# Fused attention and non-local block: a third nested product for q and k, PSUM read by halves, k's maxima in theta/phi, ScalarE for the last scaling

## The chip, the cores and the metric

The kernel runs on one NeuronCore of one Trainium2 chip. The metric is the device time of one execution in microseconds (us). The profile comes from one further execution of the same program; its span is 2154.5 us. Matrix products run on TensorE (PE in the profile, PEld for its weight loads), elementwise work and reductions on VectorE (DVE), activations and copies on ScalarE (ACT), some products and the accumulating DMAs on GpSimd (POOL), and the DMA queue is fed by SyncE (SP).

## The reference, cut to what matters

There are two layers over eight images of 512 channels and 32 x 32 positions, all in float32. The first is attention with eight heads over 1024 positions, with 1x1 convolutions for q, k, v and the output. The second is a non-local block, followed by a normalization over the whole batch.

```python
# layer 0, x is (8, 512, 32, 32), heads h = 8, d = 64
q = conv1x1(x, Wq, bq); k = conv1x1(x, Wk, bk); v = conv1x1(x, Wv, bv)
attn = softmax(einsum('bhdn,bhdm->bhnm', q, k) * d ** -0.5, axis=-1)
x = x + conv1x1(einsum('bhnm,bhdm->bhdn', attn, v), Wp, bp)
# layer 1, C_INTER = 256, n = 1024
g_x, theta_x, phi_x = (conv1x1(x, w, b) for w, b in (g, theta, phi))
y = einsum('bcd,bdn->bcn', einsum('bcn,bdn->bcd', theta_x, phi_x) / n, g_x)
z = conv1x1(y, W_w, W_b) + x
mean, var = z.mean((0, 2, 3)), z.var((0, 2, 3))      # over all eight images
out = (z - mean) * rsqrt(var + 1e-5) * gamma + beta
```

The mean and the variance need all eight images, so no output can be written before the last image's z is there.

## The kernel before: the parts that the change touches

A 512 x 512 convolution over 1024 positions is taken as a product of two 2 x 2 block matrices and done with seven block products in place of eight (the Winograd form of Strassen's scheme). Blocks of the weights are 256 x 256, blocks of the data 256 channels x 512 positions. `w[:, i]` holds the seven weight blocks: 0 is a11, 1 is a12, 2 is a22, 3 to 6 are the sums s1 to s4; t1 to t4 are the sums of data blocks, made on VectorE. Each entry of `SEVEN` is a product: its weight block, its data block, the PSUM slot that it accumulates in, and the output quarters that read the slot after it. A slot is two PSUM banks, and there are four, rotated through the list `free`.

```python
    SEVEN = (("11", 0, "11", 0, (("11", True),)), ("s1t1", 3, "t1", 1, (("22", True),)),
             ("s2t2", 4, "t2", 0, (("12", True),)), ("s4", 6, "22", 1, (("12", False),)),
             ("s3t3", 5, "t3", 0, (("22", False),)), ("12", 1, "21", 2, (("11", False),)),
             ("t4", 2, "t4", 0, (("21", True),)))
...
    FIVE = (SEVEN[0], SEVEN[1], SEVEN[2], SEVEN[3], ("s3t3", 5, "t3", 0, (("22", False), ("21", False))))
```

For q and k (images 1 to 7) and for the output projection (images 1 to 6) two of the seven, `("12", 1, "21")` and `("t4", 2, "t4")`, are left out of the list, which makes it `FIVE`, and are done by seven products again, of half the size in each direction: 128 x 128 weights with 256 positions. That is `nested`. From the second product of the list on, one such step is given to TensorE after each plain matmul, and each step is followed by one read of its PSUM slot, by VectorE (`add`) or ScalarE (`first`, where the target is written for the first time).

```python
    INNER = (1, 2)
...
    def nested(name, stage, w, data, tags, first, add):

        slots = [bank(tag, f"{name}_in_{tag}") for tag in tags]
        for n, (q, di, begins) in enumerate((("11", "21", False), ("21", "t4", True))):
            a, d = inner_blocks(w, stage, n), data[f"inner {di}"]
            pair = slots if n == 0 else slots[::-1]
            begun = set()
            for _, wi, di, s, reads in SEVEN:
                ps = pair[s % 2 if s < 2 else 1][:, s // 2, n * 256:(n + 1) * 256]
                pe(nc.tensor.matmul(ps, a[wi], d[di], start=s not in begun, stop=True, skip_group_check=True))
                ...   # the reads of this slot, then:
                yield

    def seven(name, w, data, positions_out, first, add, between=None, early=False,
              by_chunk=False, inner=None):
        ...
        for n, (what, wi, di, s, reads) in enumerate(FIVE if inner else EARLY if early else SEVEN):
            ...
            for to_ps, at, lhsT, rhs, k in work:          # four matmuls 128x512, or eight 128x256
                pe(nc.tensor.matmul(to_ps, lhsT(k), rhs(k), start=(s, at) not in begun, stop=(k == nk - 1),
                                    skip_group_check=True))
                begun.add((s, at))
                if n:
                    next(steps, None)
            for to, is_first in reads:
                (first if is_first else add)(to, ps)
            if between and n in between:
                between[n]()
```

`pe` and `dve` pin an instruction to program order on its engine; what is not pinned is placed by the scheduler. `block` gives out a tile of 128 x 1024 from a ring of ten, which also holds the exponentials of the attention, the sums t1 to t4 and the inner sums.

After q, k and v of the next image come the projection and then theta and phi of the current one. The maxima of |q| and |k| (`peaks`, four reductions over 1024 each) go into `bound_scores`, which has a small matmul, pinned on TensorE after product 3 of theta/phi, and gates q ahead of the next attention:

```python
        def peaks():
            for c in range(CC):
                ins = nc.vector.tensor_reduce(peak[:, c:c + 1], t[:, c, :], AX.X, ALU.max, apply_absolute_value=True)
                if b == 0:
                    dve(ins)
...
    def bound_scores(b, q, k, peak_q, peak_k):

        nc.vector.tensor_tensor(peak_q, peak_q, peak_k, ALU.mult)
        ps = next_bank(f"bound_{b}")[:, 0, :]
        pe(nc.tensor.matmul(ps[:, :CC], heads, peak_q, start=True, stop=True))
...
        if not last:                                       # in the loop over the images
            inner_sums(nxt["data"], "21", dve)
            more_sums(nxt["data"], (3, 4), dve)
            later = []
            q, peak_q = heads_of(b + 1, "q", ..., inner="WqT", later=later,
                                 between={1: lambda: inner_sums(nxt["data"], "t4", dve)})
            v = values(b + 1, ..., {1: norm, 2: later[0], 5: lambda: nxt["products"]()})

            def sums_of_o():
                nxt["o"] = data_sums(quarters_of(o), f"o_{b}")
                if b:
                    inner_sums(nxt["o"], "21")

            k, peak_k = heads_of(b + 1, "k", ..., inner="WkT", between={2: sums_of_o})
            if b:
                inner_sums(nxt["o"], "t4")
        ...
        tp = theta_phi(b, weights("tp"), data, {} if last else {3: lambda: bound_scores(b + 1, q, k, peak_q, peak_k)})
```

The end, where three images get their z late, channel chunk by channel chunk (`oc`), and every chunk of all eight images is scaled and written:

```python
    def last_z():
        order = [B - LATE, B - 1, *range(B - LATE + 1, B - 1)]
        begun = None
        for oc in range(CC):
            for n, b in enumerate(order[:-1] if oc == 0 else order):
                for h0, h1 in ((0, 1), (1, 2)) if (oc, n) == (CC - 1, LATE - 1) else ((0, NH),):
                    finish_one = n == 0 and begun
                    late_unit(b, oc, h0, h1, (lambda: finish(oc - 1, *begun)) if finish_one else lambda: None)()
            begun = begin(oc)
        finish(CC - 1, *begun)
...
        for i, b in enumerate(sorted(z)):                  # in finish(oc, gs, shift)
            t = z[b][oc]
            if i == 0 or oc == CC - 1 and i % 2 == 0:
                dve(nc.vector.tensor_scalar(t, t, gs, shift, ALU.mult, ALU.add))
            else:
                nc.scalar.activation(t, t, AF.Identity, bias=shift, scale=gs)
            nc.sync.dma_start(out_v[b, :, oc, :], t)
```

Of the kernel before, what the change touches and what calls it, by code (L numbers as in the profile page):

```python
# [30 lines left out]
def unshifted(ctx: ExitStack, tc: tile.TileContext, a: dict, out: bass.AP):  # L31
# [22 lines left out]
    fold1 = ctx.enter_context(tc.tile_pool(name="fold1", bufs=1))  # L54
# [59 lines left out]
    INNER = (1, 2)  # L114
    WIDTH = 7 * C + len(INNER) * 3 * P
# [40 lines left out]
    def inner_blocks(w, name, n):  # L156

        a = w[:, INNER[n]]
        extra = rest[name][:, n * 3 * P:(n + 1) * 3 * P].rearrange("p (i f) -> p i f", i=3)
        return [a[:, 0, :P], a[:, 1, :P], a[:, 1, P:], a[:, 0, P:], extra[:, 0], extra[:, 1], extra[:, 2]]  # L160

    def keep_inner(name, w):

        for n in range(len(INNER)):
            a11, a12, a22, a21, s2, s3, s4 = inner_blocks(w, name, n)
            for to, l, r, op in ((s3, a11, a21, ALU.subtract), (a21, a21, a22, ALU.add), (s2, a21, a11, ALU.subtract),
                                 (s4, a12, s2, ALU.subtract)):
                nc.vector.tensor_tensor(to, l, r, op)
        kept[name] = dram.tile([P, WIDTH], F32, tag=f"kept_{name}", name=f"kept_{name}")
        nc.sync.dma_start(kept[name][:, :14 * w.shape[3]], w.rearrange("p i k f -> p (i k f)"))  # L170
        nc.sync.dma_start(kept[name][:, 14 * w.shape[3]:], rest[name])
# [30 lines left out]
    def inner_sums(data, which, pin=lambda ins: None):  # L202

# [3 lines left out]
        pin(nc.vector.tensor_tensor(t[:, 0], b12, b11, ALU.subtract))  # L207
        pin(nc.vector.tensor_tensor(t[:, 1], b22, t[:, 0], ALU.subtract))
        pin(nc.vector.tensor_tensor(t[:, 2], b22, b12, ALU.subtract))
        pin(nc.vector.tensor_tensor(t[:, 3], b21, t[:, 1], ALU.subtract))  # L210
        data[f"inner {which}"] = {"11": b11, "21": b21, "22": b22, **{f"t{i + 1}": t[:, i] for i in range(4)}}

# [14 lines left out]

    def nested(name, stage, w, data, tags, first, add):

        slots = [bank(tag, f"{name}_in_{tag}") for tag in tags]  # L230
        for n, (q, di, begins) in enumerate((("11", "21", False), ("21", "t4", True))):
            a, d = inner_blocks(w, stage, n), data[f"inner {di}"]
            pair = slots if n == 0 else slots[::-1]
            begun = set()
            for _, wi, di, s, reads in SEVEN:
                ps = pair[s % 2 if s < 2 else 1][:, s // 2, n * 256:(n + 1) * 256]
# [8 lines left out]
    def seven(name, w, data, positions_out, first, add, between=None, early=False,  # L245
              by_chunk=False, inner=None):
# [7 lines left out]
        steps = iter(())  # L254
# [3 lines left out]
        for n, (what, wi, di, s, reads) in enumerate(FIVE if inner else EARLY if early else SEVEN):  # L258
# [14 lines left out]
            for to_ps, at, lhsT, rhs, k in work:  # L273
# [3 lines left out]
                if n:  # L277
                    next(steps, None)
            for to, is_first in reads:
                (first if is_first else add)(to, ps)  # L280
# [64 lines left out]
    def heads_of(b, what, w, bias, data, pin=lambda ins: None, later=None, **how):  # L345
# [18 lines left out]
        def peaks():  # L364
            for c in range(CC):
                ins = nc.vector.tensor_reduce(peak[:, c:c + 1], t[:, c, :], AX.X, ALU.max, apply_absolute_value=True)
                if b == 0:
                    dve(ins)
# [35 lines left out]
    def attention(b, q, k, v, near_end, make_f=None):  # L404
# [66 lines left out]
        def spread(u, pin=lambda ins: None, meanwhile=lambda: None):  # L471
# [4 lines left out]
            if not make_f:  # L476
                acc = accs.pop(u).rearrange("p j n -> p (j n)")
                if u == 0:
                    folded["t"] = foldp.tile([P, 4, 1024], F32, tag="fold", name=f"fold_{b}")
                t = folded["t"]  # L480
                together(t[i * P // 4:(i + 1) * P // 4, g, :],
                         [acc[k * P // 4:(k + 1) * P // 4, :] for k in range(4)])
                if i == 3:
                    two = t[:, g, :].rearrange("(r s) n -> s r n", s=2)
                    together(t[g * D:(g + 1) * D, 2, :], [two[0], two[1]])
                if u == len(units) - 1:
                    folded["all"] = t[:, 2, :]
                return
            if i == 0:
                folded[g] = foldp.tile([P, 4, 1024], F32, tag="fold", name=f"fold_{b}_{g}")  # L490
            acc = accs.pop(u).rearrange("p j n -> p (j n)")
            for k in range(4):
                eng = nc.scalar if make_f and u == len(units) - 1 and k % 2 else nc.sync
                eng.dma_start(folded[g][i * P // 4:(i + 1) * P // 4, k, :], acc[k * P // 4:(k + 1) * P // 4, :])
            if i == 3:
                t = folded[g]
                meanwhile()
                if g == 0:
                    folded[g] = fold1.tile([P, 1, 1024], F32, tag="fold1", name=f"fold1_{b}")
                for part_of in fold_parts(g, t, pin):  # L500
                    part_of()

        def fold_parts(g, t, pin):
            return [lambda to=to, l=l, r=r: pin(nc.vector.tensor_tensor(to, l, r, ALU.add)) for to, l, r in (
                (t[:, 0], t[:, 0], t[:, 1]), (t[:, 2], t[:, 2], t[:, 3]), (folded[g][:, 0], t[:, 0], t[:, 2]))]

        def all_denominators(ps):

            t = folded.pop("all")
# [8 lines left out]
        def denominators(g, ps):  # L518

            t = folded.pop(g)  # L520
            columns(ps, folds, lambda j: t[:, 0, j * 512:(j + 1) * 512])
            alone = make_f and g == 1
            ri = (fold1.tile([P, 1, 1024], F32, tag="fold1", name=f"ri_{b}") if alone else t)[:, 0, :512]
            nc.vector.reciprocal(ri, ps)
            if alone:
# [187 lines left out]
    def late_unit(b, oc, h0=0, h1=NH, meanwhile=lambda: None):  # L713
# [9 lines left out]
        def sums():  # L723
# [3 lines left out]
            meanwhile()  # L727
# [3 lines left out]
        return sums  # L731

    def last_z():
        order = [B - LATE, B - 1, *range(B - LATE + 1, B - 1)]
        begun = None
        for oc in range(CC):
            for n, b in enumerate(order[:-1] if oc == 0 else order):
                for h0, h1 in ((0, 1), (1, 2)) if (oc, n) == (CC - 1, LATE - 1) else ((0, NH),):
                    finish_one = n == 0 and begun
                    late_unit(b, oc, h0, h1, (lambda: finish(oc - 1, *begun)) if finish_one else lambda: None)()  # L740
            begun = begin(oc)
        finish(CC - 1, *begun)
# [8 lines left out]
    def finish(oc, gs, shift):  # L751
# [4 lines left out]
        for i, b in enumerate(sorted(z)):  # L756
            t = z[b][oc]
            if i == 0 or oc == CC - 1 and i % 2 == 0:
                dve(nc.vector.tensor_scalar(t, t, gs, shift, ALU.mult, ALU.add))
            else:  # L760
                nc.scalar.activation(t, t, AF.Identity, bias=shift, scale=gs)
            nc.sync.dma_start(out_v[b, :, oc, :], t)
# [26 lines left out]
    for b in range(B):  # L789
# [5 lines left out]
        def near_end():  # L795
            if not last:
                nxt["data"] = data_sums(quarters_of(nxt["x"]), f"x_{b + 1}", (1, 2))
            elif "data" not in nxt:
# [11 lines left out]
        if not last:  # L810
            inner_sums(nxt["data"], "21", dve)
            more_sums(nxt["data"], (3, 4), dve)
            later = []
            q, peak_q = heads_of(b + 1, "q", weights("WqT"), bq, nxt["data"], dve, inner="WqT",
                                 later=later,
                                 between={1: lambda: inner_sums(nxt["data"], "t4", dve)})
# [13 lines left out]
            k, peak_k = heads_of(b + 1, "k", weights("WkT"), bk, nxt["data"], inner="WkT", between={2: sums_of_o})  # L830
# [3 lines left out]
        else:  # L834
# [3 lines left out]
            between = {4: late_unit(b - 1, 0)}  # L838
# [21 lines left out]
        tp = theta_phi(b, weights("tp"), data, {} if last else {3: lambda: bound_scores(b + 1, q, k, peak_q, peak_k)})  # L860
        load_w(nc.sync)

        def before_wf():
            if last:
                z[b] = [xt[:, cc, :] for cc in range(CC)]
                take_back(B - LATE + 1)
                reload(4, mats, "o")
# [232 lines left out]
```

## Time and profile before

| | before |
|---|---|
| time, median of 3 | 2156.76 us (2156.75 to 2157.21) |
| span of the profiled execution | 2154.5 us |
| TensorE busy | 2128.9 us |
| VectorE busy | 1356.6 us |
| ScalarE busy | 741.4 us |
| one image in the steady part, from one q stage to the next | 264.4 us |

A matmul in float32 appears as two records in the profile, so "x8" in a line of 128x512 matmuls stands for four of them. An instruction's line gives its start and its duration; on VectorE the next one can start a little ahead of the end that is given, so the distance between two starts is the cost in a sequence. Times of TensorE are best read from start to start too[...].

### The profile page before, as it was taken

The page shows a single profiled execution, that of the slowest core. Times are in us where ns is not written, and L with a number is a line of the kernel's source. Part 1 is how long each engine was busy: PE and PEld are TensorE (multiplying, and loading weights), DVE is VectorE, ACT ScalarE, POOL GpSimd, SP SyncE. Part 2 cuts the span into 40 slices and gives each one's busy share as a digit, 9 for nine tenths or more (in the row PEclk, how much of TensorE's full clock was granted, in tenths as well). Part 3 has the DMA queues.
Part 4 walks back from the last instruction along what each step waited for, and adds up shares of the span by engine and source line. Part 5 has one row for each costly group of instructions (what it writes and reads, how often), then busy time and mean ns, then how long its engine had stood idle before and what let it go on. Part 6 is the DMA issues. An engine that isn't in the chain of part 4 may idle for free.

```text
span 2154.5 us, 29726 instructions
## 1 busy us (share of the span) xinstructions
PE 2128.9 (99%) x12426; PEld 1106.9 (51%) x12426; DVE 1356.6 (63%) x1562; ACT 741.4 (34%) x848; POOL 184.9 (9%) x235
## 2 busy tenths in 40 slices
PE   9999999999999999999999999999999999999995
PEld 4534664356733567335663366633666336643462
DVE  5466656666476664766747667476673665657736
ACT  1464104631046310463105621066212652056115
POOL 0111100110001100011000100011000110000000
PEclk9999999999999999999999999999999999999998
DMA  6333434333143331433323342233434334121648
GB/s 217 130 46 59 140 152 126 49 76 118 69 130 50 74 116 68 133 50 79 108 97 109 49 96 99 91 106 50 103 141 147 43 46 133 52 65 40 223 183 351
DMA packets 52941, 226.80 MB, mean 105 GB/s; under 512 B 9664, under 2 KB 16064, under 8 KB 45248
## 3 DMA queue, kind: packets, MB, share of 16 engines
q1 hardware_dynamic: 42128, 197.82, 27.4%
q0 software_dynamic: 9184, 25.70, 9.9%
q8 instruction: 99, 1.62, 0.3%
q10 hardware_dynamic: 1488, 1.32, 0.2%
q14 instruction: 42, 0.34, 0.1%
HBM read 138.03 MB, written 45.88 MB: 85 GB/s over the span
## 4 chain that ended last, share of the span: by engine, by line
PE 98%; DVE 1%; ACT 1%; DMA 0%; issue 0%
PE ps L430 20%; PE po L456 20%; PE pv L274 9%; PE ptp L274 9%; PE pp L274 7%; PE pk L274 7%; PE pq L274 6%; PE pg L274 4%; PE pf L609 3%; PE pz L274 2%; PE pk_in_s L237 2%; PE pq_in_s L237 2%; PE pp_in_s L237 2%; PE pz L720 2%; PE pwf L644 1%; PE den L402 0%
## 5 line engine op out<-in xcount | busy, mean ns | idle before, releaser
L433 ACT ACTIVATE e<-ps 128x1024 f32<-128x1024 f32 x512 | 522.9, 1025 | 428.0 <-PE ps L430 422.5
L439 DVE TENSOR_TENSOR acc<-acc,e 128x1024 f32<-128x1024 f32 x384 | 470.0, 1224 | 141.9 <-ACT e L433 137.3
L456 PE MATMUL po<-e,v 64*64 64x512 f32 x4096 | 528.7, 589 | 0.7 <-ACT w_WgT L611 0.7
L430 PE MATMUL ps<-q,k 64*64 64x512 f32 x4096 | 529.1, 589 | 0.0
L456 PEld LDWEIGHTS po<-e,v 64*64 64x64 f32 x4096 | 156.4, 133 | 283.5 <-issue 275.4
L430 PEld LDWEIGHTS ps<-q,k 64*64 64x64 f32 x4096 | 155.5, 133 | 284.1 <-issue 275.1
L469 POOL DMA_DIRECT2D fold<-acc x168 | 131.1, 780 | 893.1 <-DMA fold<-acc 562.7
L437 DVE TENSOR_TENSOR acc<-e,e 128x1024 f32<-128x1024 f32 x64 | 78.3, 1224 | 139.6 <-ACT e L433 132.9
L632 ACT ACTIVATE g<-pg,gb 128x512 f32<-128x512 f32 x31 | 21.3, 687 | 384.1 <-PE pg L274 381.3
L274 PE MATMUL pv<-w_WvT,t_x 128*128 128x256 f32 x512 | 116.4, 381 | 0.0
L274 PE MATMUL ptp<-w_tp,t_x 128*128 128x256 f32 x512 | 115.0, 380 | 0.0
L274 PEld LDWEIGHTS pv<-w_WvT,t_x 128*128 128x128 f32 x512 | 96.6, 190 | 18.5 <-issue 5.7
L274 PEld LDWEIGHTS ptp<-w_tp,t_x 128*128 128x128 f32 x512 | 96.7, 190 | 12.9
L274 PE MATMUL pp<-t_o,w_WpT 128*128 128x512 f32 x208 | 100.8, 592 | 0.0
L274 PE MATMUL pq<-t_x,w_WqT 128*128 128x512 f32 x200 | 98.8, 593 | 1.0 <-DVE w_WqT L772 1.0
L274 PE MATMUL pk<-t_x,w_WkT 128*128 128x512 f32 x200 | 98.9, 592 | 0.0
L385 ACT COPY v<-pv 128x1024 f32<-128x1024 f32 x32 | 32.4, 1012 | 185.2 <-PE pv L274 185.2
L397 POOL TENSOR_SCALAR q<-q,gates 128x1024 f32<-128x1024 f32 x32 | 35.2, 1111 | 659.8 <-DVE gates L395 659.8
L274 PE MATMUL ptp<-w_tp,x 128*128 128x256 f32 x384 | 86.8, 379 | 0.0
L274 PE MATMUL pv<-w_WvT,x 128*128 128x256 f32 x384 | 86.8, 379 | 0.0
L274 PEld LDWEIGHTS ptp<-w_tp,x 128*128 128x128 f32 x384 | 73.0, 190 | 13.3 <-issue 3.6
L274 PEld LDWEIGHTS pv<-w_WvT,x 128*128 128x128 f32 x384 | 73.0, 190 | 13.3 <-issue 3.6
(187 smaller groups left out, 2191.0 us busy)
## 6 DMA issues: line engine op xcount, KB each, us to landing
fold<-acc POOLq DMA_DIRECT2D x168, 128.0 KB, 3.1
r<-den_d SPq DMA_DIRECT2D x32, 512.0 KB, 6.9
x<-in_x_dram SPq DMA_DIRECT2D x31, 512.0 KB, 6.0
w_WqT<-kept_WqT SPq DMA_DIRECT2D x7, 2176.0 KB, 8.9
w_WkT<-kept_WkT SPq DMA_DIRECT2D x7, 2176.0 KB, 8.7
w_WpT<-kept_WpT SPq DMA_DIRECT2D x6, 2176.0 KB, 8.4
w_WvT<-kept_WvT SPq DMA_DIRECT2D x7, 1792.0 KB, 7.2
w_tp<-kept_tp SPq DMA_DIRECT2D x7, 1792.0 KB, 8.5
```

Of the source, the lines that this page charges most:

```text
L237: pe(nc.tensor.matmul(ps, a[wi], d[di], start=s not in begun, stop=True, skip_group_check=True))
L274: pe(nc.tensor.matmul(to_ps, lhsT(k), rhs(k), start=(s, at) not in begun, stop=(k == nk - 1), skip_group_check=True))
L385: seven(f"pv_{b}", w, data, True, lambda q, ps: nc.scalar.copy(at(q), as_v(ps)), lambda q, ps: dve(nc.vector.tensor_tensor(at(q), at(q), a ...
L397: nc.gpsimd.tensor_scalar(q[:, p, :], q[:, p, :], gate[:, p:p + 1], 1.0, ALU.mult, ALU.mult)
L430: pe(nc.tensor.matmul(ps[c * P // 2:(c + 1) * P // 2, j, :], k[r, p, keys], q[r, p, h * 512:(h + 1) * 512], start=True, stop=True, skip_gr ...
L433: nc.scalar.activation(e, ps, AF.Exp, scale=SCALE)
L437: nc.vector.tensor_tensor(accs[u], es[u, 0], e, ALU.add)
L439: ins = nc.vector.tensor_tensor(accs[u], accs[u], e, ALU.add)
L456: pe(nc.tensor.matmul(ps[j * D:(j + 1) * D, r, :], v[keys, m, (2 * p + j) * D:(2 * p + j + 1) * D], e[keys, j, :], start=(m == 0), stop=(m ...
L469: nc.gpsimd.dma_start(to, part_of, accum_op=ALU.add)
L609: pe(nc.tensor.matmul(ps[:, c, :], tp[:, i, c * P:(c + 1) * P], tp[:, i, CI:], start=(i == 0), stop=(i == NB - 1)))
L720: pe(nc.tensor.matmul(ps[:, h - h0, :], wf[:, d, oc * P:(oc + 1) * P], g[d][:, h * 512:(h + 1) * 512], start=(d == 0), stop=(d == IC - 1), ...
```

## The change

A third of the seven products of q and k, s4 times b22, is also done by seven smaller ones; the output projection keeps two. With that the plain list of q and k shrinks from `FIVE` to `FOUR`, in which s1t1 is read into both quarters 22 and 12. Their plain slots are read as soon as each half (128 x 512) is complete. `STEPS` says how many nested steps follow each plain matmul. The VectorE sums are placed at given matmuls of the q stage by `fills`, and one more set of inner sums, of b22, is made at the end of the attention. k's maxima move from the end of the k stage into theta/phi, after product 1; the sums of o move from after product 2 to after product 1 of the k stage. At the end, the oldest late chunk is done ahead of the last image's Wf, each channel chunk is finished as soon as its statistics are there, and its first image is scaled by ScalarE in two halves (in the last chunk VectorE keeps every other image). Two smaller parts are in the denominators: in the last image the folding of the sums uses accumulating DMAs for all units but the last, as it does in the other images, and a buffer (`fold1`) goes.

```diff
-    INNER = (1, 2)
-    WIDTH = 7 * C + len(INNER) * 3 * P
+    INNER = {"WqT": (1, 6, 2), "WkT": (1, 6, 2), "WpT": (1, 2)}
+    WIDTH = 7 * C + 3 * 3 * P
...
+    FOUR = (SEVEN[0], ("s1t1", 3, "t1", 1, (("22", True), ("12", True))), ("s2t2", 4, "t2", 0, (("12", False),)),
+            FIVE[4])
+    STEPS = {2: [0] * 4 + [1] * 14, 3: [0, 0, 1, 1, 0, 1, 1, 2, 2, 2, 2, 2, 2, 2, 2, 1]}
...
-        for n, (q, di, begins) in enumerate((("11", "21", False), ("21", "t4", True))):
+        goes_to = {1: ("11", "21", False), 6: ("12", "22", False), 2: ("21", "t4", True)}
+        for n, (q, di, begins) in enumerate(goes_to[i] for i in INNER[stage]):
...
-            pair = slots if n == 0 else slots[::-1]
+            pair = slots[::-1] if n % 2 else slots
...
-                if n:
-                    next(steps, None)
-            for to, is_first in reads:
+                if three and k == nk - 1 and n < 3:
+                    read(reads, ps, at)
+                for _ in range(next(counts, 0)):
+                    next(steps)
+                if three and k == nk - 1 and n == 3:
+                    read(reads, ps, at)
+                if unit in fills:
+                    fills[unit]()
+                unit += 1
+            for to, is_first in () if three else reads:
                 (first if is_first else add)(to, ps)
...
-                if b == 0:
+                if b == 0 or later is not None:
                     dve(ins)
...
     def last_z():
         order = [B - LATE, B - 1, *range(B - LATE + 1, B - 1)]
-        begun = None
         for oc in range(CC):
-            for n, b in enumerate(order[:-1] if oc == 0 else order):
+            for n, b in enumerate(order if oc else [B - 1]):
                 for h0, h1 in ((0, 1), (1, 2)) if (oc, n) == (CC - 1, LATE - 1) else ((0, NH),):
-                    finish_one = n == 0 and begun
-                    late_unit(b, oc, h0, h1, (lambda: finish(oc - 1, *begun)) if finish_one else lambda: None)()
-            begun = begin(oc)
-        finish(CC - 1, *begun)
+                    late_unit(b, oc, h0, h1)
+            finish(oc, *begin(oc))
...
-            if i == 0 or oc == CC - 1 and i % 2 == 0:
-                dve(nc.vector.tensor_scalar(t, t, gs, shift, ALU.mult, ALU.add))
-            else:
-                nc.scalar.activation(t, t, AF.Identity, bias=shift, scale=gs)
-            nc.sync.dma_start(out_v[b, :, oc, :], t)
+            for at in (slice(0, 512), slice(512, N)) if i == 0 and oc < CC - 1 else (slice(0, N),):
+                if oc == CC - 1 and i % 2 == 0:
+                    dve(nc.vector.tensor_scalar(t[:, at], t[:, at], gs, shift, ALU.mult, ALU.add))
+                else:
+                    nc.scalar.activation(t[:, at], t[:, at], AF.Identity, bias=shift, scale=gs)
+                nc.sync.dma_start(out_v[b, :, oc, at], t[:, at])
...
                 nxt["data"] = data_sums(quarters_of(nxt["x"]), f"x_{b + 1}", (1, 2))
+                inner_sums(nxt["data"], "22")
...
-            more_sums(nxt["data"], (3, 4), dve)
-            later = []
+            later, of_t4 = [], []
+            fills = {4: lambda: more_sums(nxt["data"], (3,), dve), 5: lambda: more_sums(nxt["data"], (4,), dve),
+                     9: lambda: (of_t4.extend(inner_parts(nxt["data"], "t4", dve)), of_t4[0](), of_t4[1]()),
+                     10: lambda: (of_t4[2](), of_t4[3]())}
...
-            k, peak_k = heads_of(b + 1, "k", weights("WkT"), bk, nxt["data"], inner="WkT", between={2: sums_of_o})
+            later_k = []
+            k, peak_k = heads_of(b + 1, "k", weights("WkT"), bk, nxt["data"], later=later_k, inner="WkT",
+                                 between={1: sums_of_o})
...
-        tp = theta_phi(b, weights("tp"), data, {} if last else {3: lambda: bound_scores(b + 1, q, k, peak_q, peak_k)})
+        tp = theta_phi(b, weights("tp"), data, {} if last else
+                       {1: later_k[0], 3: lambda: bound_scores(b + 1, q, k, peak_q, peak_k)})
...
         def before_wf():
             if last:
+                late_unit(B - LATE, 0)
                 z[b] = [xt[:, cc, :] for cc in range(CC)]
+                reload(4, mats, "o")
                 take_back(B - LATE + 1)
-                reload(4, mats, "o")
```

## The prediction

> **What bounds the kernel.** The page comes first, with busy time by engine and the chain that ended last.
>
> ```profile
> PE 2128.9 (99%) x12426; PEld 1106.9 (51%) x12426; DVE 1356.6 (63%) x1562; ACT 741.4 (34%) x848; POOL 184.9 (9%) x235
> ...
> PE 98%; DVE 1%; ACT 1%; DMA 0%; issue 0%
> ```
>
> TensorE is the chain, so removed matmul time is worth its full length and every wait of TensorE costs its full length. "99%" does not prove that there are no waits, so the second view is TensorE's timeline of a stage that is changed, k of image 2:
>
> ```profile
> 503.47 3.60 PE L274 MATMUL pk<-x,w_WkT 128*128 128x512 f32 x8
> 506.90 1.02 PE L274 MATMUL pk<-t_x,w_WkT 128*128 128x512 f32 x2
> 507.76 0.59 PE L237 MATMUL pk_in_s<-x,w_WkT 128*128 128x256 f32 x2
> 508.19 1.02 PE L274 MATMUL pk<-t_x,w_WkT 128*128 128x512 f32 x2
> ...
> 526.68 3.60 PE L274 MATMUL pp<-o,w_WpT 128*128 128x512 f32 x8
> ```
>
> From start to start a 512-wide matmul takes 0.86 us and a 256-wide one 0.43. The stage, 20 plain matmuls and 14 nested steps, should take 20 x 0.858 + 14 x 0.43 = 23.18; it takes 526.68 - 503.47 = 23.21. It is free of waits. So each nested step's read of PSUM was always in time.
>
> Third view, VectorE in the same image at theta/phi, the new home of k's maxima:
>
> ```profile
> 552.36 1.22 DVE L200 TENSOR_TENSOR t_x<-x,t_x 128x1024 f32<-128x1024 f32 x1
> 553.54 1.22 DVE L594 TENSOR_TENSOR tp<-ptp,tpb 128x1024 f32<-128x1024 f32 x1
> 554.69 1.22 DVE L200 TENSOR_TENSOR t_x<-x 128x1024 f32<-128x1024 f32 x1
> 555.82 1.22 DVE L200 TENSOR_TENSOR t_x<-x,t_x 128x1024 f32<-128x1024 f32 x1
> 557.00 1.23 DVE L594 TENSOR_TENSOR tp<-ptp,tpb 128x1024 f32<-128x1024 f32 x1
> 560.45 1.23 DVE L594 TENSOR_TENSOR tp<-ptp,tpb 128x1024 f32<-128x1024 f32 x1 [2.23 <-PE ptp L274]
> ```
>
> Up to 558.1 VectorE has no gap here, and then it has about 2.2 us free in each product of 3.45 us.
>
> Fourth view, the end: the output queue's issues, and the engines in stretches of 2 us (busy time of PE, PEld, DVE, ACT, POOL, then clock, DMA share, GB/s).
>
> ```profile
> 2107.99 5.44 SPq L762 DMA_DIRECT2D out_dram<-z  x6
> ```
>
> ```profile
> 2106.00:2108.00 2.00, 2.00 (x6) 0.92 (x5) 1.89 (x6) 0.80 (x1) 0.00 (x0) 1.00 0.01 4
> 2108.00:2110.00 2.00, 2.00 (x6) 0.93 (x5) 2.00 (x3) 2.00 (x3) 0.00 (x0) 1.00 0.61 244
> 2110.00:2112.00 2.00, 2.00 (x6) 0.80 (x6) 1.63 (x3) 2.00 (x3) 0.00 (x0) 1.00 1.02 404
> ...
> 2148.00:2150.00 2.00, 0.00 (x0) 0.00 (x0) 0.00 (x0) 0.00 (x0) 0.00 (x0) 0.50 1.04 416
> 2150.00:2152.00 2.00, 0.00 (x0) 0.00 (x0) 0.00 (x0) 0.00 (x0) 0.00 (x0) 0.50 0.28 109
> ```
>
> The output is 8 x 512 x 1024 x 4 bytes = 16.8 MB. From 2108.6 to 2150.5 all DMA engines are busy at some 400 GB/s, and 16.8 MB / 400 GB/s = 42 us. So the end is set by when the first output is issued, whatever the engines do after it.
>
> [...] the last product stage of z, 596.64 to 609.20, counts as fully busy, but its 14 matmuls need 12.0 of those 12.56 us. [...] 1.22, 0.68 and 0.42 us for 1024, 512 and 256 elements, 1.13, 0.6 and 0.34 from start to start; reading PSUM by halves costs VectorE only 0.06 more per pair. [...] with scale and bias as pointers this trace shows 1.15 from start to start. [...]
>
> **Part 1, the third nested product.** It replaces four 512-wide matmuls (3.43 us) by seven 256-wide ones (3.01), so each q and k stage loses 0.43 us. Seven images have two such stages: 14 x 0.43 = -6.0 us.
>
> The price is density. With one step after each plain matmul, two steps on the same slot lay 2 x 0.86 + 0.43 us apart; with two steps per matmul only 0.86 + 0.43 = 1.29 us are left for the read in between. I put the two stages through by hand with the trace's durations, VectorE's instructions in the order in which they stand in the built program, 0.2 us from the end of a matmul's issue to the start of its read (461.75 + 0.43 to 462.38) and 0.1 from the end of a read to TensorE (DVE read ended at 603.79, matmul started at 603.90). **q** comes out without a wait: its sums are spread by `fills`, and VectorE is busy some 10 of the 14 us in which steps come in pairs.
>
> **k** does not. One more tile (inner sums of b22) now lives in the ring of ten, and the sums of o are asked for one product earlier. So t4 of o gets the place of t1 of x, which the fifth to eighth plain matmul of the stage still read, and the inner sums of o get the place of the inner sums of x, which step 6 still reads: in the built order both have a wait on TensorE that they did not have before. Counted from the start of the stage: t4 of o starts at 8.8 and ends at 9.9, the read of step 4 ends at 10.35, and step 6 starts at 10.46 in place of 10.30 (0.16 us). It ends at 10.9; then VectorE has three inner sums (3 x 0.34), the read of step 6 (0.34), a fourth sum (0.34) and the read of step 7, which ends at 13.2. Step 9, due at 12.6, accumulates on the slot that this read frees and starts at 13.3 (0.72 us). So 0.88 us for each of images 2 to 7, 5.3 us, and in image 1, where other sums stand there, about 0.5: +5.8 us.
>
> **Part 2, k's maxima in theta/phi.** At the end of the k stage they cost TensorE nothing, so nothing is gained. In theta/phi they come after the read of product 1: four reductions from 558.14 at 1.13 each end at 562.7; then the read of product 2 is done, 1.14; the product of the maxima is ready at 563.96; TensorE can have the bound matmul at 564.07. Before, it stood at 563.70. So TensorE waits 0.37 us in each of seven images: +2.6 us.
>
> **Part 3, the end.** Before, the first scaling waited behind one addition of z (1.28 us) and took 0.81 on VectorE; from the statistics' end at 2104.48 to the issue at 2107.99 it took 3.5. In the last chunk, where nothing stood between, the same chain took 1.63 us up to ScalarE's first activation (2135.02 to 2136.65). With a half chunk of 0.7 this makes 2.4: the first issue comes 1.1 us sooner, and the end with it. Eight activations of 1.15 are 9.2 us per chunk, less than the 10.4 that its 4.2 MB take, so ScalarE feeds the queue: -1.1 us. Moving one late unit ahead of Wf changes only the order of TensorE's work.
>
> The other parts are off the path: the denominators' sums of the last image keep three additions, and 9% more kept weights load beside a stage of 23 us.
>
> Sum: 2156.8 - 6.0 - 1.1 + 5.8 + 2.6 = 2158.1.
>
> **Rivals.** (a) *The saving arrives whole*: VectorE serves reads and sums in time, as it did before; then 2156.8 - 7.1 = 2149.7. For it speak the free VectorE time in the profile and the care of `fills`; against it the two new waits in the built order. (b) *Only one of the waits is real*: without that of k 2152.3, without that of the bound matmul 2155.5. The latter is likelier to be there, as it is read from a dense stretch of the trace; the former hangs on where two waits of a few tenths fall. (c) *Density becomes the bound*: the q stage waits too, some 0.4 us in seven images, and the reads of image 1 collide with the sums of Wp: 2161 or more. (d) *The end is not moved*: the chunks come 10.3 us apart from TensorE and take 10.4 on the queue, so a gap of a few tenths between chunks could eat the gain: 2159.
>
> **Range and chances.** I give my sum most weight, (a) and (b) together a good third, (c) and (d) the rest, and shade the sum by 1.6 us: 2156.5 us, 8 in 10 between 2150.5 and 2160.5. Even (a) is 0.3%, so within 2% is nearly certain: faster by over 2% 0.01, within 2% 0.98, slower by over 2% 0.01.
>
> **What would show it.** In the new profile the k stage of images 2 to 7 should take 23.6 us from start to start, with one longer gap between nested steps just after its middle; 22.75 would speak for (a). The q stage should take 22.8, 23.2 for (c). Before the bound matmul TensorE should stand still for about 0.4 us. The first output issue should come 2.4 us after the statistics of the first chunk, and the queue should then be full for 42 us. The prediction is wrong if the k stage has no wait, or if waits come in stages that I take as untouched (v, projection, attention).

## The result, and the profile after

The changed kernel takes 2227.43 us (median of 6 runs, 2227.18 to 2227.74), the kernel before 2156.91 beside it: a ratio of 1.0327, 95% interval 1.0314 to 1.034. It is 70.5 us slower, where 2156.5 was predicted. The profiled spans, 2225.7 and 2154.5 us, differ by 71.2.

The first and the fourth part of the page, busy time and the chain that ended last:

```profile
PE 2147.2 (96%) x12510; PEld 1114.8 (50%) x12510; DVE 1407.9 (63%) x1732; ACT 747.3 (34%) x854; POOL 201.7 (9%) x256
...
PE 87%; DVE 7%; ACT 3%; DMA 1%; issue 1%; SPq 0%; DVEq 0%; ACTq 0%
```

TensorE was 98% of the chain and is now 87%: it waits for VectorE and ScalarE. The view of TensorE's waits names them (instruction, what released it, then us in total, times, longest):

```profile
PE pq L290 <- ACT q L376: 12.6, 14, 1.1
PE pq L290 <- DVE q L316: 12.5, 7, 1.8
PE pk L290 <- DVE k L316: 12.2, 13, 1.3
PE pk L290 <- ACT k L376: 11.9, 14, 0.9
PE pk_in_s L246 <- DVE k L316: 1.7, 7, 0.4
PE bound L416 <- DVE peak_q L414: 1.2, 6, 0.2
```

The last two are the waits that the prediction expected. The first four, on the *plain* matmuls of q and k, it did not: 49 us of visible idle, and more from start to start (the first wait below is listed with 0.78, from start to start it is 0.94). Where they stand is seen in TensorE's timeline of the k stage of image 2:

```profile
517.34 1.88 PE L290 MATMUL pk<-x,w_WkT 128*128 128x512 f32 x4
520.00 1.12 PE L290 MATMUL pk<-x,w_WkT 128*128 128x512 f32 x2 [0.78 <-ACT k L376]
520.96 0.59 PE L246 MATMUL pk_in_s<-x,w_WkT 128*128 128x256 f32 x2
...
525.91 1.12 PE L290 MATMUL pk<-t_x,w_WkT 128*128 128x512 f32 x2 [0.92 <-ACT k L376]
...
532.20 1.37 PE L246 MATMUL pk_in_s<-i_x,w_WkT 128*128 128x256 f32 x4 [0.23 <-DVE k L316]
534.08 1.13 PE L290 MATMUL pk<-t_x,w_WkT 128*128 128x512 f32 x2 [0.51 <-DVE k L316]
...
542.72 1.13 PE L290 MATMUL pk<-t_x,w_WkT 128*128 128x512 f32 x2 [1.31 <-DVE k L316]
```

Each product has four plain matmuls, two per half. The first product shows it best: two matmuls from 517.34, which complete half 0, and then the third, the first of half 1, should come at 519.06 (two times 0.86) and comes at 520.00. It is released by ScalarE's read of half 0, which ScalarE's timeline has at 519.26, 0.69 long:

```profile
519.26 0.69 ACT L376 ACTIVATE k<-pk,bk 128x512 f32<-128x512 f32 x1 [0.71 <-PE pk L290]
```

Half 1 waits until half 0 has been *read*. All four products do this, by 0.94, 1.08, 0.68 and 1.47 us from start to start, 4.17 in all. Some 0.73 lie around the nested steps at 532.20 (0.39 ahead of them and 0.34 inside the group of two, 1.37 in place of 1.03), and 0.8 in gaps of about 0.1, mostly after a wait. With 22.78 us of work that is the stage's 28.5.

Stages from start to start in a steady image, in us, with the sum over the seven images:

| stage | before | after | sum of the difference |
|---|---|---|---|
| q | 23.31 | 27.76 (27.82 and 28.13 in images 2 and 7) | +31.6 |
| v | 25.38 | 25.38 | 0 |
| k | 23.21 | 28.50 (27.87 in image 1) | +36.4 |
| projection, attention | 23.21, 110.03 | 23.21, 110.03 | 0 |
| theta/phi | 24.40 | 24.84 | +3.0 |
| last image's sums and projection | | | +0.9 |
| the end, from the first chunk's statistics | 50.02 | 49.34 | -0.7 |

The sum is 71.2, the whole difference. VectorE in theta/phi, and TensorE at the bound matmul, stand as predicted:

```profile
576.15 1.22 DVE L604 TENSOR_TENSOR tp<-ptp,tpb 128x1024 f32<-128x1024 f32 x1
577.30 4.59 DVE L389 TENSOR_REDUCE peak_k<-k 128x1 f32<-128x1024 f32 x4
581.80 1.21 DVE L604 TENSOR_TENSOR tp<-ptp,tpb 128x1024 f32<-128x1024 f32 x1
582.93 0.15 DVE L414 TENSOR_TENSOR peak_q<-peak_q,peak_k 128x4 f32<-128x4 f32 x1
```

```profile
579.41 3.62 PE L290 MATMUL ptp<-w_tp,x 128*128 128x256 f32 x16
583.23 0.35 PE L416 MATMUL bound<-peak_q,heads 128*128 128x4 f32 x2 [0.21 <-DVE peak_q L414]
```

Product 3 started at 579.41 and needs 3.45 (16 records, 8 matmuls of 0.43); the bound matmul came at 583.23, 0.37 late. Then the end: the queue's issues, and stretches of 2 us counted from the end of the first chunk's statistics at 2176.36 (columns as before):

```profile
2178.83 6.70 SPq L771 DMA_DIRECT2D out_dram<-z  x7
```

```profile
2178.36:2180.36 2.00, 2.00 (x6) 0.86 (x5) 1.97 (x3) 2.00 (x3) 0.00 (x0) 1.00 0.34 127
2180.36:2182.36 2.00, 2.00 (x6) 0.95 (x5) 1.83 (x3) 2.00 (x3) 0.00 (x0) 1.00 0.81 315
2182.36:2184.36 2.00, 2.00 (x6) 0.84 (x5) 1.17 (x3) 2.00 (x3) 0.00 (x0) 1.00 1.02 406
...
2220.36:2222.36 2.00, 0.00 (x0) 0.00 (x0) 0.00 (x0) 0.00 (x0) 0.00 (x0) 0.50 0.83 332
```

The first issue comes 2.47 us after the statistics (predicted 2.4, before 3.5): 1.63 up to ScalarE's first activation at 2177.99, and then 0.84, of which the half chunk itself lasts 0.81. The prediction's 0.7 for it was the author's estimate; a 128x512 activation with a bias alone lasts 0.69 (519.26 above). But the queue is not full then: 0.34 and 0.81 in the next stretches, where the kernel before had 0.61 in its stretch of the first issue and then 1.02.

### The profile page after: what moved, and what is told of

Same layout as the page of the kernel before. It is cut to its first block, busy times and chain, and to the rows that moved or that the text cites. A ratio compares the mean times of both kernels' runs of the same rounds, so it can differ in the third digit from the quotient of the medians.

```text
span 2225.7 us, 30171 instructions
## 1 busy us (share of the span) xinstructions
PE 2147.2 (96%) x12510; PEld 1114.8 (50%) x12510; DVE 1407.9 (63%) x1732; ACT 747.3 (34%) x854; POOL 201.7 (9%) x256
## 4 chain that ended last, share of the span: by engine, by line
PE 87%; DVE 7%; ACT 3%; DMA 1%; issue 1%; SPq 0%; DVEq 0%; ACTq 0%
PE ps L453 20%; PE po L479 20%; PE pv L290 9%; PE pp L290 6%; PE pk L290 6%; PE pq L290 5%; PE ptp L290 4%; PE pg L290 4%; PE pf L619 2%; PE pk_in_s L246 2%; PE pz L290 2%; PE pq_in_s L246 2%; PE pp_in_s L246 2%; DVE peak_k L389 1%; PE pwf L654 1%; ACT z L770 1%
## 5 line engine op out<-in xcount | busy, mean ns | idle before, releaser
L492 POOL DMA_DIRECT2D fold<-acc x189 | 147.1, 779 | 1009.7 <-DMA fold<-acc 575.7
L316 DVE TENSOR_TENSOR q<-q,pq_in_s 128x256 f32<-128x256 f32 x119 | 48.7, 419 | 65.0 <-PE pq_in_s L246 34.0
```

The costliest lines, as they stand in the source:

```text
L316: pin(nc.vector.tensor_tensor(at, at, ps if len(ps.shape) == 3 else ps.unsqueeze(1), ALU.add))
L492: nc.gpsimd.dma_start(to, part_of, accum_op=ALU.add)
```

## The experiments

The theory (T1): a slot is one PSUM tile of two banks, and the program guards it as a whole, so that a matmul into half 1 waits for the read of half 0. The built program says so by itself: the third matmul below, the first of half 1, waits for ScalarE (Activation), which reads half 0; in the trace it is the one with 0.78 us of wait at 520.00. This is TensorE's order in the k stage of image 2 (the number behind a name is the tile; "waits" names the engine whose semaphore it waits for):

```
656 L290 Matmult pk_2_0_0_2840<-x_2_1814,w_WkT_2748 128x512 [waits DMAHW5_49,PE_49]
657 L290 Matmult pk_2_0_0_2840<-x_2_1814,w_WkT_2748 128x512
658 L290 Matmult pk_2_0_0_2840<-x_2_1814,w_WkT_2748 128x512 [waits Activation_49]
```

The main rival (R1): density. The reads, doubled in number and squeezed into less time, come too late whatever the guard. Below, "before" is 2156.61 us beside the first four runs, 2156.84 beside the next four and 2156.88 beside the last two.

**The halves in alternating tiles.** The changed kernel, with half m of every product in tile m, in its bank s, in place of half m in bank m of tile s. TensorE's work and every read stay; while half 0's tile is read, half 1 goes into another tile.

```diff
-  parts = [(ps[:, m, :], m, ...
+  parts = [(slots[m][:, s, :] if three else ps[:, m, :], m, ...
-  (first if is_first else add)((slice(c, c + 1), cols(to)), ps[:, m, :])
+  (first if is_first else add)((slice(c, c + 1), cols(to)), slots[m][:, s, :])
```

> The changed kernel with one difference: of each plain product of q and k the first half goes into one PSUM tile and the second half into another, so that the halves that follow each other lie in different tiles. Number, order and size of matmuls, steps and reads are the same. Theory T1 (a PSUM tile is guarded as a whole, so the second half's matmul waits for the read of the first half): the waits before the third and seventh matmul of the stage go, the q stage takes 22.8 to 23.3 us in place of 27.8, the k stage 23 to 24 in place of 28.5, and the time is 2150 to 2160. Rival R1 (two nested steps per matmul are too dense for VectorE): little changes, above 2200. Rival R2 (places in the ring of ten make VectorE and TensorE wait for each other): the k stage stays above 26, the q stage hardly changes.

Measured: 2183.39 us, ratio 1.0124 (1.0107 to 1.0141); q 24.44, k 25.24. This is 23 us above T1's range and 17 below R1's. R2 falls, since q is 3.3 us shorter. The view of waits keeps none of a plain matmul of q or k for a read. What is left stands at the end of each stage, where v begins in the tile that was read last; here after the q stage of image 2:

```profile
481.05 0.59 PE L246 MATMUL pq_in_s<-i_t_x,w_WqT 128*128 128x256 f32 x2
483.02 3.26 PE L294 MATMUL pv<-w_WvT,x 128*128 128x256 f32 x14 [1.38 <-DVE q L320]
```

So 44 of the 70.5 us (2227.43 - 2183.39) were the guard inside the stage.

**Halves alone.** The kernel before, with two nested products, plain slots read by halves in q, k and the projection. No density is added.

```diff
+  if inner and k == nk - 1:
+      for to, is_first in reads:
+          c = rows(to).start + at
+          (first if is_first else add)((slice(c, c + 1), cols(to)), ps[:, at, :])
-  for to, is_first in reads:
+  for to, is_first in () if inner else reads:
```

> The kernel before with one difference: the plain products of q, k and the projection with inner products are read as soon as each half is complete, with two nested products as before. T1: each of the five products gets a wait ahead of its second half, about 1.05 us for the first (no step between), 0.6 for the next three and 1.1 for the last with its two reads, 4 us per stage; 14 stages of q and k and 6 of the projection make up to 80, so 2205 to 2240. R1 and R2: no third product, no denser steps, one tile less in the ring, so 2157 as before.

Measured: 2250.40 us, ratio 1.0434 (1.0417 to 1.0452). The stages that took 23.3, 23.2 and 23.2 take 27.91 (q), 27.38 (k) and 28.63 (projection); the waits sit on the same plain matmuls:

```profile
PE pp L274 <- DVE x L580: 14.4, 18, 1.6
PE pq L274 <- DVE q L297: 12.1, 14, 1.3
PE pq L274 <- ACT q L357: 11.0, 21, 1.1
PE pk L274 <- ACT k L357: 10.3, 21, 0.8
```

My bound of 2240 was too low: I took 4 us per stage, and it is 4.6 in q, 4.2 in k and 5.4 in the projection. Of the 94 us lost, some 62 lie in q and k: reading by halves alone brings a loss of nearly the size of the 69 us that the guard costs in the changed kernel, without any third product.

**Whole reads.** The changed kernel, with both halves of a slot read only after the product's fourth matmul, and the nested steps shifted by one matmul at the start.

```diff
-  STEPS = {..., 3: [0, 0, 1, 1, 0, 1, 1, 2, 2, 2, 2, 2, 2, 2, 2, 1]}
+  STEPS = {..., 3: [0, 0, 0, 1, 1, 1, 1, 2, 2, 2, 2, 2, 2, 2, 2, 1]}
-  if three and k == nk - 1 and n < 3:
-      read(reads, ps, at)
+  if three and unit % 4 == 3 and n < 3:
+      read(reads, ps, 0)
+      read(reads, ps, 1)
...                                                    # the same for the last product, after its steps
```

> The changed kernel with the plain products of q and k read whole, both halves after the last matmul of a product, and one nested step moved from the third matmul to the fourth (and one from the fourth on) so that nothing is added before its target is written. T1: the waits ahead of second halves go; a new one comes ahead of the fourth product, which takes the slot of the third and waits for two reads (about 0.7 us in 14 stages), so 2160 to 2170. R1: the steps are as dense as in the changed kernel, so above 2200.

Measured: 2172.35 us, ratio 1.0071 (1.0054 to 1.0088); q 23.83, k 24.51; the whole is 2 us above T1's range and far below R1's. One wait per stage remains on the plain matmuls, ahead of the fourth product, where the slot of the third is taken again while it is still being read:

```profile
PE pq L290 <- DVE q L318: 4.6, 7, 0.7
PE pk L290 <- DVE k L318: 3.6, 7, 0.5
PE pk_in_s L246 <- DVE k L318: 1.8, 7, 0.4
```

With this tile, late reads are 55 us better than the halves that were meant to be earlier, and the number of reads is the same.

**k's maxima and the end alone**, on the kernel before (its q and k stages untouched).

```diff
-  if b == 0:
+  if b == 0 or later is not None:
       dve(ins)
...
-  k, peak_k = heads_of(..., inner="WkT", between={2: sums_of_o})
+  k, peak_k = heads_of(..., later=later_k, inner="WkT", between={2: sums_of_o})
...
+  {1: later_k[0], 3: lambda: bound_scores(b + 1, q, k, peak_q, peak_k)})
```

> The kernel before with k's maxima in theta/phi and the new end, nothing else: two nested products, whole reads. My step for the maxima: TensorE waits 0.37 us ahead of the bound matmul in seven images, +2.6; the end brings 0.7 (seen in the changed kernel: 49.34 us from the first chunk's statistics to the end, against 50.02). So 2158.7. If the maxima were free: 2156.1.

Measured: 2159.59 us, ratio 1.0014 (1.0007 to 1.002); theta/phi 24.84 in place of 24.40, and q, v, k and the projection of images 1 to 6 the same. The prediction's sum for these two parts, +2.6 - 1.1 = 1.5, was about half of the 3.0 seen. In this trace the end gave nothing: 49.98 us from the statistics to the span's end, against 50.02.

**The other hand-over.** The alternating tiles, and the next stage starts in a tile that was read long before.

```diff
-  free[:] = [tags[1], tags[2], tags[3], tags[0]]
+  free[:] = [tags[3], tags[2], tags[0], tags[1]] if three else [tags[1], tags[2], tags[3], tags[0]]
```

> The alternating tiles of the run before, and in the stages with three nested products the order of the free slots at the stage's end is changed, so that the next stage begins in a tile that was read long before, and the two tiles read last come after it. Theory (each tile of two banks is guarded as a whole; the last 1.4 to 1.6 us per stage are the hand-over of the tile read last): q 22.8 us, k 23.5 (the ring's wait of 0.7 to 0.8 stays), v 25.4, theta/phi 24.84, and 2157 to 2160 us in all, which is the prediction's own sum of 2158.1 with the guard taken out. Rival (the rest of the loss is density, the reads coming too late for TensorE by themselves): q and k stay at 24.4 and 25.2, and 2180 or more.

Measured: 2163.13 us, ratio 1.0028 (1.0017 to 1.0038); q 22.90, k 23.74, v 25.38. In the steady images R1 falls: all 21 nested steps of q fit in, without a wait. The whole is 3 us above my range. Image 1, where the sums of Wp are made, has a k stage of 24.47 us, and from the small matmuls of its bias to the projection it takes 1.73 in place of 0.81; the view of waits has them wait for GpSimd's products of bias and weights.

**Sums of o one product later**, on that version:

```diff
-  between={1: sums_of_o})
+  between={2: sums_of_o})
```

> As the run with the other hand-over, and the sums of o are asked for after product 2 of the k stage again, not after product 1. Theory (k's extra time over q is the ring's wait for the sums of o): k falls to 22.8 to 23.0, the same as q, and the whole is about 5 us (0.75 x 7) below that run: 2152 to 2155. Rival (k's extra time is VectorE's load, not the ring): k stays within 0.2 us of that run, and so does the whole within 1.5 us.

Measured: 2156.94 us, ratio 1.0003 (0.9995 to 1.0011); k 22.99 in place of 23.74. The whole is 2 us above the range, and 6.2 below that run where 5 were expected; the profiled spans differ by 4.8. TensorE's timeline of the k stage in image 2, first with the early sums and then with the late ones:

```profile
516.84 1.02 PE L294 MATMUL pk<-t_x,w_WkT 128*128 128x512 f32 x2
518.09 1.36 PE L246 MATMUL pk_in_s<-i_x,w_WkT 128*128 128x256 f32 x4 [0.23 <-DVE k L320]
519.29 1.02 PE L294 MATMUL pk<-t_x,w_WkT 128*128 128x512 f32 x2
```

```profile
516.38 1.02 PE L294 MATMUL pk<-t_x,w_WkT 128*128 128x512 f32 x2
517.24 1.03 PE L246 MATMUL pk_in_s<-i_x,w_WkT 128*128 128x256 f32 x4
518.11 1.02 PE L294 MATMUL pk<-t_x,w_WkT 128*128 128x512 f32 x2
```

From the plain matmul to the next one it is 2.45 us, then 1.73. With a smaller gap beside it that is the extra 0.75 us per stage. VectorE's order in the two built programs shows what the edit changed. With the early sums, three inner sums of o wait for step 6, which reads what had their place in the ring, and the read of step 6 comes after them (in the changed kernel's trace, which has the same order there, they start at 530.72 and the read at 531.73). With the late sums, this read comes first. The place in the ring is not what was taken away: t4 of o waits for the same matmul of TensorE in both programs. The same sums fit in another order, so VectorE's load as such is not the cause; its order and the ring were not tried apart.

**k's maxima back at the end of the k stage**, on the version with the other hand-over (the reverse of the edit for the maxima above):

> As the run with the other hand-over, and k's maxima are made at the end of the k stage again. Theory (the maxima in theta/phi cost 0.44 us per image at the bound matmul and gain nothing): theta/phi 24.40, k unchanged, the whole about 3 us below that run: 2154 to 2157. Rival (at the end of the k stage they now stand in the way of the reads, which are denser than before): k 0.3 us or more longer, and the whole the same as that run or above it.

Measured: 2159.0 us, ratio 1.0011 (1.0004 to 1.0017); theta/phi 24.40 again, k 23.74 unchanged. The move cost 0.44 us an image and gained nothing. The range was too low by 2 us, that of the run it was built on by 3.

**Both back** (late sums and old maxima):

> As the run with the other hand-over, with both taken back: sums of o after product 2 and k's maxima at the end of the k stage. Theory: both savings add, q and k 22.8, theta/phi 24.40, and 2149.5 to 2152 us, some 6 us below the kernel before (14 x 0.43 = 6.0, and up to 1 of the end): rival (a) of the prediction, the saving that arrives whole. Rival (density): with sums and maxima both late in the k stage VectorE falls behind there, k stays at 23.2 or more, and the whole is 2153 or above.

Measured: 2153.68 us, ratio 0.9986 (0.998 to 0.9993), faster than both kernels, by 3.2 us against the one before. The steady stages are q 22.90, k 22.99, theta/phi 24.40, so the third product now gives 0.41 us per q stage and 0.22 per k stage, where two gaps of 0.1 remain. The whole is still above my range: image 1 loses 1.8 (its k stage 24.10 in place of 23.21, the bias 1.73 in place of 0.81), and the end gives less than I took.

**The end alone**, on the kernel before (the last part of the change's diff, `last_z`, `finish` and `before_wf`):

> The kernel before, with the end of the changed kernel alone (oldest late chunk ahead of Wf, each chunk finished at once, its first image scaled by ScalarE in halves). Theory (the first issue comes 1.0 to 1.1 us sooner after the statistics, but ScalarE alone cannot fill the queue in the first 4 us, where the kernel before had two engines scaling): first issue 2.47 us after the statistics, DMA share about 0.3 and 0.8 in the next two stretches of 2 us where before it was 0.86 at once, and 0.4 to 0.7 us gained in all, 2156.2 to 2156.5. Prediction's step (the end moves with the first issue): 1.1 us, 2155.7. Rival (d) of the prediction (a gap between the chunks eats it): a stretch with a DMA share below 0.9 between chunks, and no gain.

Measured: 2156.76 us, ratio 1.0001 (0.9992 to 1.0009), no difference that could be told. The stretches from the end of the statistics at 2104.54 show why; the first issue is at 2107.01, 2.47 us after it:

```profile
2106.54:2108.54 2.00, 2.00 (x6) 0.86 (x5) 1.97 (x3) 2.00 (x3) 0.00 (x0) 1.00 0.34 127
2108.54:2110.54 2.00, 2.00 (x6) 0.95 (x5) 1.83 (x3) 2.00 (x3) 0.00 (x0) 1.00 0.81 315
2110.54:2112.54 2.00, 2.00 (x6) 0.84 (x5) 1.17 (x3) 2.00 (x3) 0.00 (x0) 1.00 1.02 406
...
2148.54:2150.54 2.00, 0.00 (x0) 0.00 (x0) 0.00 (x0) 0.00 (x0) 0.00 (x0) 0.50 0.78 313
```

The issue is 1.04 us earlier, but the first two pieces are halves, a quarter MB each, made by one engine one after the other, where in the kernel before VectorE and ScalarE each began with a whole image of the chunk. So the queue is full only from 2110.5. Taking each share as the part of its stretch that was busy, the transfers end at 2148.54 + 2 x 0.78 = 2150.1, 45.6 us after the statistics; in the kernel before at 2148.48 + 2 x 0.94 = 2150.4, 45.9 after them (its stretch is the line below). So 0.3 us is gained, and from 2110.54 to 2148.54 no stretch has a share below 1.0: rival (d)'s gap between chunks is not there. From the end of the transfers to the span's end it is 4.5 us here and 4.1 before, which takes back what was won.

```profile
2148.48:2150.48 2.00, 0.00 (x0) 0.00 (x0) 0.00 (x0) 0.00 (x0) 0.00 (x0) 0.50 0.94 371
```

**Two engines at a chunk's start**, on the fastest version: the second half of a chunk's first image goes to VectorE.

```diff
-  if oc == CC - 1 and i % 2 == 0:
+  if oc == CC - 1 and i % 2 == 0 or at.start == 512:
```

> The fastest version so far (alternating tiles, other hand-over, sums of o and k's maxima in their old places, new end), with one thing changed: in each of the first three chunks the second half of the first image is scaled by VectorE, not ScalarE, so that two engines start a chunk. Theory (the queue starves at the start of a chunk since one engine feeds it): DMA share above 0.5 in the stretch of the first issue (0.34 in that version) and full in the next, 0.3 to 0.6 us less, some 2153.2. Rival (VectorE is held by the additions and statistics of the next chunk, which come first in its order): the second half comes late, the queue is no fuller, and the time is the same or up to 0.5 us longer.

Measured: 2154.3 us, ratio 0.9987 (0.9981 to 0.9994): in time the same as without it, and 1 us above what was expected. In the trace the queue does fill sooner, with the statistics' end at 2102.55:

```profile
2104.55:2106.55 2.00, 2.00 (x6) 0.86 (x5) 1.97 (x3) 2.00 (x3) 0.00 (x0) 1.00 0.49 182
2106.55:2108.55 2.00, 2.00 (x6) 0.95 (x5) 1.97 (x4) 2.00 (x3) 0.00 (x0) 1.00 1.02 401
...
2146.55:2148.55 2.00, 0.00 (x0) 0.00 (x0) 0.00 (x0) 0.00 (x0) 0.00 (x0) 0.50 0.59 236
```

The share is 0.49 and then full, and the transfers end 45.2 us after the statistics, without the edit 45.6. The starved start is confirmed by the shares; what it is worth, 0.4 us, is below what these times can tell.

## Why the prediction was wrong, point by point

**The step that failed** is "I put the two stages through by hand", with its result that "q comes out without a wait". The walk has waits for the slots of the nested steps and for the ring, and none of a plain matmul for the read of the other half. The program guards the tile of two banks, so the first matmul of half 1 waits for the read of half 0, in every product of every q and k stage. That is 4.9 us per q stage (27.76 against the 22.88 of 23.31 - 0.43) and, with the ring's 0.75 taken off, 5.0 per k stage (28.50 - 22.78 - 0.75): 69 us in fourteen stages. The alternating tiles took the waits inside the stage away, the other hand-over the rest, and halves alone brought them back without a third product, so the cause is shown and not only argued. The halves of a slot lie in different banks, but the guard was one per tile: in the trace above half 1 comes 0.68 to 1.47 us late in all four products. That the kernel before kept the second half's work going did not speak against it: there the read came after both halves.

**Part 1, the saving.** Right in size once the guard is out: 0.41 us per q stage of the 0.43, in k 0.22.

**Part 1, the ring.** Right in place and near in size: 0.75 us per k stage for 0.88, removed by the later sums of o alone. As the prediction had it, three inner sums of o stood ahead of the read of step 6; the ring's part in this was not shown apart from VectorE's order. Image 1 was mis-sized: 0.5 was predicted for its k stage, but with the guard out the stage is 1.7 us over its 22.78, and the bias's wait for GpSimd adds 0.9. Later sums of o take 0.45 of that back (24.02 for 24.47), and moving the maxima nothing (24.50). Of the rest, the trace of the version with both back shows one wait of 0.58 us from start to start (259.21 in place of 258.63), for a read that comes on VectorE right behind a sum of Wp's weights. That sum lasts 1.47 us, where the one of its size at 252.72 lasts 0.28, and the 32 in the changed kernel's trace 0.28 or 0.29:

```profile
257.35 1.47 DVE L168 TENSOR_TENSOR w_WpT<-w_WpT 128x128 f32<-128x128 f32 x1
258.74 0.41 DVE L320 TENSOR_TENSOR k<-k,pk_in_s 128x256 f32<-128x256 f32 x1
259.21 0.70 PE L246 MATMUL pk_in_s<-t_x,w_WkT 128*128 128x256 f32 x2 [0.41 <-DVE k L320]
```

Why this one took so long was not shown, and no run has the sum in another place.

**Part 2, the bound matmul.** The wait was 0.37 us as predicted; the stage grew by 0.44, since the matmul that follows then starts 0.22 us after it, where it was 0.14 before. Seven images make 3.0 for 2.6.

**Part 3, the end.** "The first issue comes 1.1 us sooner" was right (1.04), "and the end with it" was not: the queue starts half fed, and 0.3 us remain in the transfers.

**The sum.** 2158.1 was the prediction for a kernel without the guard. That kernel was measured at 2163.1 (2161.4 to 2163.8). Its profiled span is 5.1 us above that of before, where the sum had 1.3. Of these 3.8, 2.1 lie in image 1 (k 24.47 for 23.28, and the bias 0.9), 0.5 in the other k stages (23.74 for 23.66), 0.4 in theta/phi, 0.4 at the end, and 0.4 are spread. The other 1.2 us show in the timed runs alone: five of the eight lie at 2162.9 to 2163.8 us, and three, the profiled one among them, at 2161.4 to 2161.7. A longer stretch that could be the reason stands in the trace of the run with the maxima back at the end of the k stage. In image 1, right after the bias's wait, the projection takes 5.20 us there from its first matmul to its fifth (263.19 to 268.39), in place of 3.52 in the trace of the kernel without the guard (263.20 to 266.72); here the four matmuls, first of this kernel and then of that run:

```profile
263.20 3.68 PE L294 MATMUL pp<-o,w_WpT 128*128 128x512 f32 x8
```

```profile
263.19 5.37 PE L294 MATMUL pp<-o,w_WpT 128*128 128x512 f32 x8
```

That is 1.7 us. What made these matmuls longer is not shown, nor that the longer timed runs of the kernel without the guard have it too.

**The rivals.** (a) came nearest only once the guard was out and two of the moves were undone; (b) falls, both waits are real; (c) falls for the steady images, since q has no wait at full density, but its part on image 1 came true, where more was lost than the sum had; (d) had the result and not the mechanism. None had the guard, and "within 2%" at 0.98 rested on all of them sharing the same walk. The last sentence of the prediction looked for waits in the stages taken as untouched, and they came in the very stages that I had walked through.

## What to carry to other kernels

Before a buffer is read in parts so that the rest can be filled meanwhile, look in the built order at what the first writer of the next part waits for: if the buffer is one tile, reading early can make the writer wait earlier (here 4.9 us per q stage), and each part needs a tile of its own (or parts alternate between tiles, which took q here from 27.76 to 24.44). A new schedule is best walked through with the built program's waits, every one of them, and not with those that the data need. And where a queue sets the end, count when it is *full*, not when it begins: here an issue 1.04 us earlier brought the end of the transfers 0.3 us.

## What was not expected

Reading a product's halves as soon as each was complete was slower than reading both after the last matmul, by 55 us over fourteen stages (2227.43 and 2172.35). Each of the four waits of plain matmuls in the k stage of image 2 cost a little beyond its length: the matmul that ends it takes 0.96 or 0.97 us to the next one in place of 0.86 (the first 520.00 to 520.96). And from the last busy DMA stretch to the end of the span it took 3.7 to 4.5 us in six of these kernels, a spread nearly as large as the 1.1 us that the end was to bring.
